# Layer 1: where the two upper halves stand among the involutions and the second convolution

## The chip, the cores and the metric

One Trainium2 chip, one of its cores. The metric is the time of one execution in device microseconds, the median of several runs. Lower is better.

## What is computed

Input `x` has 16 images of 16 channels of 256 x 256 values, in float32. Layer 0 is a spectral operator, layer 1 a convolutional gate; both work on a group-normed input and add their result to it. Only layer 1 is changed:

```python
xs = x.reshape(B * C, 1, H, W)
f = mish(conv2d(xs, W1, b1))                      # 4 features per channel, 3x3
top, bot = (f[:, :, :H2], f[:, :, H2:])           # upper and lower half of the rows
ker = conv2d(relu(conv2d(bot, Wred, bred)), Wspan, bspan)
top_inv = (patches(top) * ker[:, None]).sum(axis=2)   # involution
bo = bot.reshape(B, C, 4, H2, W)
shuffled = concatenate([ti, roll(bo, -1, axis=1)], axis=3)
out = mish(conv2d(shuffled, W2, b2))              # 64 -> 16 channels, 3x3
pooled = out.mean(axis=(2, 3))
gate = sigmoid(Weca[0] * left + Weca[1] * mid + Weca[2] * right)
return x * gate[:, :, None, None]
```

## The kernel before

The program runs layer 0 in three parts and then layer 1 (`layer1`, line 933). The change touches layer 1's main loop alone (lines 1288 to 1329).

**Units.** An image is cut into nine units (`blocks`, line 1268): eight of 30 output rows and eight channels, and a tail of eight rows and all channels. A unit holds up to two groups of four channels; the tail has one. `Unit` has these steps:

- Making it loads its two inputs `z` (lower and upper half) from `zn` in DRAM on SP's queue (`load_rows`, line 1006).
- `lower` (line 1050): per group two matmuls into a PSUM tile `c` (`conv1`, line 1037), and two ScalarE activations into `bot` (line 1056).
- `reduce` (line 1058): four small matmuls into `pr` (line 1064), two ScalarE relus into `r` (line 1073), and the stores of `bot` to `cf` from GpSimd's queue (line 1157).
- `upper(g)` (line 1076), g = 0 and 1: the two matmuls of a group into `c`, and eight ScalarE activations of 32 lanes into `wide` (line 1085). For the tail, `upper(1)` does nothing.
- `spread` (line 1092): eight GpSimd copies inside `wide` (lines 1097, 1098) that need both groups of `upper`.
- `involution(f)` (line 1100), f = 0 to 3: per group one matmul into `pd` (line 1105), then on VectorE one product `t` (line 1113) and two sums `top` (line 1116). `involution(3)` issues the stores of `top` from GpSimd's queue (lines 1127 to 1139).

**Second convolution.** `conv2` (line 1167) treats one of eight slabs of the image before, in pieces between `yield`s; slab s of the image before runs in iteration s. The first piece: eight matmuls `c2ps` from `rows` (line 1185), a ScalarE copy `mid` (line 1199), a VectorE sum `pair` (line 1175). The second: sixteen matmuls from `rows`, VectorE's `even` and `both` (lines 1204, 1206), the rest of `pair`. The third: mish of `even` (line 1196), sixteen matmuls from `pair`, VectorE's `odd` (line 1212). The slab is loaded from `cf` on SP's queue (`conv2_rows`, line 1165) one iteration ahead.

**Gate.** In iteration s = 8, where there is no slab, `gate` (line 1217) makes one small matmul `pg` (line 1237) and an exp on ScalarE (line 1240), then in four steps, in iterations 8, 0, 1 and 2, scales the image on GpSimd (line 1253), with its parts loaded on SP's queue (line 1229) and stored from GpSimd's (line 1262).

**What sets the order.** The section is a manual schedule: PE, ScalarE, VectorE and GpSimd each run their instructions in the order in which the loop writes them. Iteration i works on three units at a time: `now` (unit i, its involutions), `nxt` (unit i + 1, its lower, reduce, upper, spread), and unit i + 2, whose loads are begun.

**PSUM.** Two tiles for `c` (so each `upper` or `lower` group takes the tile of the group two before it), three for `pd`, `pr` and `pg`, one for `c2ps` (in the last image's slabs also the three).

Of the kernel before, what the change touches and what calls it, by code (L numbers as in the profile page):

```python
# [932 lines left out]
def layer1(ctx, tc, d, zn, cf, mr, nb):  # L933
# [228 lines left out]
    def conv2_rows(b, s):  # L1162
        t = rows2[(8 * b + s) % 2]
        flat = cf[b % 4].rearrange("(t y) f c x -> (y f c) t x", y=2)
        nc.sync.dma_start(out=t[:, :, 1 : N + 1], in_=flat[:, 16 * s : 16 * s + 17])
# [106 lines left out]
    def begin_unit(i):  # L1272
        if i < len(order):
            b, s = order[i]
            units[i] = Unit(b, i, *blocks[s])

    E = mybir.EngineType
    with tc.manual_schedule(engines={E.PE, E.Activation, E.DVE, E.Pool}):
        begin_unit(0)
        begin_unit(1)  # L1280
        u = units[0]
        u.lower()
        u.reduce()
        u.upper(0)
        u.upper(1)
        u.spread()
        acc, last, second = None, iter(()), iter(())
        for i in range(9 * nb + 12):
            b, s = divmod(i, 9)
            now, nxt = units.pop(i, None), units.get(i + 1)  # L1290
            begin_unit(i + 2)
            if s == 8 and b < nb:
                conv2_rows(b, 0)
            if s < 7 and b and b <= nb:
                conv2_rows(b - 1, s + 1)
            if nxt:
                nxt.lower()
            next(second, None)
            second = iter(())
            if s == 8 and b and b <= nb:  # L1300
                last = gate(b - 1, acc)
                next(last)
            if s < 8 and b and b <= nb:
                if s == 0:
                    acc = sm.tile([P, 16], F32, tag="acc", name="acc")
                second = conv2(b - 1, s, acc)
            if now:
                now.involution(0)
            next(second, None)
            if nxt:  # L1310
                nxt.reduce()
            if s == 8:
                next(last, None)
            if now:
                now.involution(1)
            next(second, None)
            if nxt:
                nxt.upper(0)
            if now:
                now.involution(2)  # L1320
            if s == 8:
                next(last, None)
            if nxt:
                nxt.upper(1)
                nxt.spread()
            next(last, None)
            next(second, None)
            if now:
                now.involution(3)
# [159 lines left out]
@with_exitstack  # L1489
def forward(ctx, tc, d):  # L1490
    nb = d["x"].shape[0]
    dram = ctx.enter_context(tc.tile_pool(name="dram", bufs=1, space=DRAM))
    keep = ctx.enter_context(tc.tile_pool(name="keep", bufs=1))
    al = dram.tile([NF, 2, 64, nb, N], F32, name="al")
    bd = dram.tile([nb, P, P], F32, name="bd")
    hd = dram.tile([2, 2, 64, nb, C, N], F32, name="hd")
    tabs = (
        dram.tile([P, 2, C, N], F32, name="td"),
        dram.tile([NF, P, 384], F32, name="avd"),
        dram.tile([P, 2, C, N], F32, name="ed"),  # L1500
    )
    zn = dram.tile([nb, N + 2, C, N + 2], F32, name="zn")
    cf = dram.tile([4, N + 2, 4, C, N], F32, name="cf")
    mr = keep.tile([P, nb, G, 2], F32, name="mr")
    layer0_forward(tc, d, al, bd, tabs)
    layer0_mix(tc, d, al, hd, tabs)
    layer0_back(tc, d, hd, bd, zn, mr, tabs[2])
    layer1(tc, d, zn, cf, mr, nb)
# [25 lines left out]
```

## Time and profile before

| what | us |
|---|---|
| median of 3 runs | 7288.94 |
| lowest and highest run | 7282.32, 7289.96 |
| the profiled execution | 7272.96 |
| its span, first to last instruction | 7271.2 |

The span by stages, from an answer of the trace by stretches (busy us of each engine, TensorE's granted clock, share of the DMA engines):

| stretch, us | what runs | PE | VectorE | ScalarE | GpSimd | clock | DMA |
|---|---|---|---|---|---|---|---|
| 0 to 3560 | layer 0 | 3205.66 | 2686.58 | 1558.39 | 1343.08 | 0.98 | 0.48 |
| 3573 to 3790 | layer 1, image 0 | 174.95 | 140.53 | 138.39 | 103.31 | 0.86 | 0.58 |
| 3790 to 4010 | image 1 | 207.22 | 177.73 | 142.09 | 107.38 | 0.98 | 0.82 |
| 4010 to 7050 | images 2 to 15 | 2852.52 | 2449.04 | 1963.48 | 1870.62 | 0.98 | 0.86 |
| 7050 to 7271 | the end, conv2 and gate of the last image | 163.18 | 127.68 | 74.59 | 91.04 | 0.92 | 0.69 |

How to read the lines below: a group line has the line of the kernel, engine, operation, tiles (out<-in), shapes and count, then busy us and mean ns of one, then the idle time of the engine just before and what ended it. A timeline line has start, duration, engine, line, operation, tiles, shapes and count of merged records, and in brackets the idle time before it and who ended it. A float32 matmul leaves two records, so "x4" at line 1037 is one group. A line by stretches has the stretch, its length, busy us and counts of PE, PE's weight loads, VectorE, ScalarE and GpSimd, then clock, DMA share and GB/s. PE is TensorE, DVE VectorE, ACT ScalarE, POOL GpSimd, SP SyncE.

### The profile page before, as it was taken

How to read it: one execution, taken by the hardware profiler on the slowest of the kernel's cores; microseconds unless marked ns; L12 is line 12 of the kernel's file. 1: busy time of each engine (PE TensorE's matmuls, PEld its weight loads, DVE VectorE, ACT ScalarE, POOL GpSimd, SP SyncE). 2: the span in 40 equal slices, each digit the busy share in tenths (PEclk: the TensorE clock that was granted, in tenths of full speed). 3: DMA queues.
4: the chain of work that ended last, by engine and by line, in shares of the span. 5: the costliest groups of instructions: out<-in, count | busy, mean ns of one | idle time of the engine just before them, and what ended most of it. 6: DMA issues, size and time to landing. Idle time of an engine off the chain costs nothing.

```text
span 7271.2 us, 144305 instructions
## 1 busy us (share of the span) xinstructions
PE 6603.5 (91%) x55592; PEld 3651.8 (50%) x55592; DVE 5587.6 (77%) x10106; ACT 3876.9 (53%) x6043; POOL 3524.5 (48%) x4614
## 2 busy tenths in 40 slices
PE   7889999899999998999789999999999999999996
PEld 5767778666666766677423333333333333333332
DVE  8999985466666666788678787788877887778875
ACT  2223333466666665222366666666666666666662
POOL 2334445322222222666555666556665566665663
PEclk9899999999999999999889999999999999999999
DMA  3334444433333332999767888888888889888886
GB/s 100 114 112 125 123 120 125 123 99 99 99 96 99 98 99 87 325 325 326 242 180 225 254 269 249 254 261 258 271 244 252 256 254 275 253 247 260 253 261 229
DMA packets 716081, 1443.39 MB, mean 199 GB/s; under 512 B 98954, under 2 KB 525254, under 8 KB 673638
## 3 DMA queue, kind: packets, MB, share of 16 engines
q1 hardware_dynamic: 567206, 959.76, 44.1%
q0 software_dynamic: 148192, 474.40, 21.1%
q8 instruction: 444, 7.27, 0.4%
q14 instruction: 239, 1.96, 0.1%
HBM read 877.12 MB, written 556.47 MB: 197 GB/s over the span
## 4 chain that ended last, share of the span: by engine, by line
PE 37%; DMA 5%; ACT 4%; DVE 3%; issue 1%; POOL 0%; SPq 0%; DVEq 0%; ACTq 0%; POOLq 0%
PE c2ps L1185 14%; PE c L1037 11%; PE pd L1105 10%; ACT wide L1085 3%; DMA rows<-cf 3%; DVE top L1116 1%; PE pr L1064 1%; DMA z<-zn 1%; DVE t L1113 1%; DMA cf<-bot 0%; SPq L1017 0%; DVE pair L1175 0%; ACT L1085 0%; ACT bot L1056 0%; POOL o L1253 0%
## 5 line engine op out<-in xcount | busy, mean ns | idle before, releaser
L1085 ACT ACTIVATE wide<-c,b 32x512 f32<-32x512 f32 x2176 | 1479.0, 680 | 832.1 <-PE c L1037 768.3
L1116 DVE TENSOR_TENSOR top<-pd,t 32x512 f32<-32x512 f32 x2176 | 1504.1, 691 | 53.0 <-DMA cf<-top 0.5
L1037 PE MATMUL c<-z,w 102*128 102x512 f32 x2048 | 1046.0, 636 | 212.3 <-ACT wide L1085 190.8
L1097 POOL COPY wide<-wide 32x1031 f32<-32x1031 f32 (+1 forms) x576 | 576.0, 1000 | 1167.8 <-ACT wide L1085 1141.7
L1113 DVE TENSOR_TENSOR t<-pd,r 64x512 f32<-64x512 f32 x1088 | 744.5, 684 | 504.5 <-PE pd L1105 472.1
L1105 PE MATMUL pd<-wide,dw 128*128 128x512 f32 x2048 | 1026.4, 622 | 16.4 <-DVE top L1116 11.5
L720 POOL DMA_DIRECT2D hd<-h x512 | 324.4, 640 | 1195.9 <-DVE h L713 1170.9
L1037 PEld LDWEIGHTS c<-z,w 102*128 102x128 f32 x2048 | 384.0, 197 | 818.3 <-issue 488.8
L1185 PE MATMUL c2ps<-rows,c 128*32 128x512 f32 x6144 | 722.9, 603 | 24.6 <-DMA rows<-cf 19.0
L1105 PEld LDWEIGHTS pd<-wide,dw 128*128 128x128 f32 x2048 | 370.3, 194 | 641.6 <-issue 490.5
L1098 POOL COPY wide<-wide 32x1031 f32<-32x1031 f32 (+1 forms) x576 | 573.3, 995 | 33.7
L643 PE MATMUL ps<-tt,lt 128*64 128x256 f32 x4224 | 495.5, 384 | 13.8 <-DMA tt<-td 10.6
L700 PE MATMUL ph<-ix,yt 64*128 64x256 f32 x4128 | 500.9, 390 | 5.6 <-issue 4.8
L313 PE MATMUL px<-wxn,u 128*64 128x256 f32 x4224 | 481.7, 379 | 7.8 <-ACT o L320 7.8
L207 PE MATMUL pu<-fy,eo 128*128 128x128 f32 x2048 | 427.0, 292 | 26.5 <-DVE u L224 21.8
L1185 PEld LDWEIGHTS c2ps<-rows,c 128*32 128x32 f32 x6144 | 176.7, 109 | 533.5 <-issue 400.3
L700 PEld LDWEIGHTS ph<-ix,yt 64*128 64x128 f32 x4128 | 392.3, 190 | 92.0 <-issue 45.0
L873 POOL TENSOR_TENSOR x<-x,o 128x512 f32<-128x512 f32 x256 | 324.3, 1267 | 216.6 <-DVE o L872 197.3
L607 DVE TENSOR_SCALAR alb<-alc,m 128x1024 f32<-128x1024 f32 x330 | 420.2, 1398 | 0.0
L214 PE MATMUL pv<-at,eo 128*128 128x128 f32 x2048 | 413.7, 285 | 0.0
L651 DVE COPY s<-ps 128x512 f32<-128x512 f32 x264 | 265.7, 1024 | 189.0 <-PE ps L643 171.2
L665 PE MATMUL pg<-alb,s 128*32 128x64 f32 x16896 | 274.1, 221 | 132.3 <-issue 86.4
(217 smaller groups left out, 11785.6 us busy)
## 6 DMA issues: line engine op xcount, KB each, us to landing
rows<-cf SPq DMA_DIRECT2D x128, 2176.0 KB
z<-zn SPq DMA_DIRECT2D x768, 257.8 KB
cf<-top POOLq DMA_DIRECT2D x512, 240.0 KB, 7.0
cf<-bot POOLq DMA_DIRECT2D x96, 840.0 KB, 11.4
alc<-al SPq DMA_DIRECT2D x264, 256.0 KB
zn<-zb SPq DMA_DIRECT2D x128, 516.0 KB
o<-zn SPq DMA_DIRECT2D x128, 516.0 KB
z<-in_x SPq DMA_DIRECT2D x64, 1024.0 KB
```

Source lines behind the costliest of these rows:

```text
L207: nc.tensor.matmul(pu[:, xh, e].rearrange("p v m -> p (v m)"), lhsT=lhs, rhs=fy[:, e], start=True, stop=True,)
L313: nc.tensor.matmul(ps[64 * k : 64 * k + 64, :, h], lhsT=u[:, h, part, g0 + j + k].rearrange("p f c -> p (f c)"), rhs=wxn[:, h, part], star ...
L643: nc.tensor.matmul(ps[64 * h : 64 * h + 64, v], lhsT=lt[:, h, k, 1 - v : 3 - v].rearrange("p l f c -> p (l f c)"), rhs=tt[:, h, k], start= ...
L700: nc.tensor.matmul(ph[q][:, e], lhsT=yt[lanes, i].rearrange("p t k -> p (t k)"), rhs=ix[lanes, i], start=n == 0, stop=n == 3,)
L1037: nc.tensor.matmul(ps[:, a], lhsT=w, rhs=z[:k, c : c + 2, 0:N], start=True, stop=True)
L1085: nc.scalar.activation(self.feat[64 - 32 * q : 96 - 32 * q, f, self.groups[g], :H], ps[q][32 * f : 32 * f + 32], AF.Mish, bias=b1[0][32 * ...
L1097: nc.gpsimd.tensor_copy(flat[0:32, f, 1:m], flat[64:96, f, 0 : m - 1])
L1098: nc.gpsimd.tensor_copy(flat[96:128, f, 0 : m - 1], flat[32:64, f, 1:m])
L1105: nc.tensor.matmul(ps, lhsT=dwt if self.tail else dw, rhs=self.feat[:, f, cs, :H], start=True, stop=True,)
L1113: nc.vector.tensor_tensor(t[64:128], ps[:64], self.r[:, cs], ALU.mult)
L1116: nc.vector.tensor_tensor(self.top[32 * f : 32 * f + 32, cs, q], ps[lanes], t[lanes], ALU.add)
L1185: nc.tensor.matmul(ps[32 * j : 32 * j + 32], lhsT=w[:, blk], rhs=src[:, 4 * j + blk : 4 * j + blk + 4, x : x + H], start=(i, blk) == (0, 0 ...
```

## The change

In the loop's body `nxt.upper(0)` moves up, ahead of `now.involution(1)` and with it ahead of the second piece of conv2. `nxt.upper(1)` and `nxt.spread()` move up from behind `now.involution(2)` to ahead of it. Between the two halves there now stand one involution feature and one piece of conv2. The steps and what they compute stay the same.

```diff
             if s == 8:
                 next(last, None)
+            if nxt:
+                nxt.upper(0)
             if now:
                 now.involution(1)
             next(second, None)
             if nxt:
-                nxt.upper(0)
+                nxt.upper(1)
+                nxt.spread()
             if now:
                 now.involution(2)
             if s == 8:
                 next(last, None)
-            if nxt:
-                nxt.upper(1)
-                nxt.spread()
             next(last, None)
             next(second, None)
             if now:
                 now.involution(3)
```

## Prediction

> **What bounds the kernel now.** I read the page first. TensorE (PE) is busy for 91% of the span, and of its groups only `c` (line 1037) waits long for another engine: 190.8 us for ScalarE's `wide` activations (line 1085). Layer 0, which the change doesn't touch, ends near 3560 us.
>
> ```profile
> PE 6603.5 (91%) x55592; PEld 3651.8 (50%) x55592; DVE 5587.6 (77%) x10106; ACT 3876.9 (53%) x6043; POOL 3524.5 (48%) x4614
> L1037 PE MATMUL c<-z,w 102*128 102x512 f32 x2048 | 1046.0, 636 | 212.3 <-ACT wide L1085 190.8
> ```
>
> Then the timeline of layer 1, engine by engine. First a unit in the steady state (PE, then ScalarE): the `c` at 5604.25 is the second half of `upper`, those at 5611.46 and 5614.11 the two groups of the next `lower`. ScalarE needs 11.26 us for the sixteen `wide`; it starts when the first half lands and ends at 5614.06. The second `lower` needs the PSUM buffer of the second half, so PE idles 0.77 us.
>
> ```profile
> 5604.25 1.88 PE L1037 MATMUL c<-z,w 102*128 102x512 f32 x4
> ...
> 5611.46 1.88 PE L1037 MATMUL c<-z,w 102*128 102x512 f32 x4
> 5614.11 1.99 PE L1037 MATMUL c<-z,w 102*128 102x512 f32 x4 [0.77 <-ACT wide L1085]
> ```
> ```profile
> 5602.80 11.26 ACT L1085 ACTIVATE wide<-c,b 32x512 f32<-32x512 f32 x16 [6.00 <-PE c L1037]
> 5614.92 2.47 ACT L1056 ACTIVATE bot<-c,b 128x512 f32<-128x512 f32 x4
> ```
>
> Second, image 0, which has no second convolution yet. The same wait is 0.60 and 3.65 us, and after the long one four matmul records take 3.78 us, not 1.88: PE's clock has halved.
>
> ```profile
> 3634.54 1.88 PE L1105 MATMUL pd<-wide,dw 128*128 128x512 f32 x4
> 3637.03 1.99 PE L1037 MATMUL c<-z,w 102*128 102x512 f32 x4 [0.60 <-ACT wide L1085]
> 3642.67 3.78 PE L1037 MATMUL c<-z,w 102*128 102x512 f32 x4 [3.65 <-ACT wide L1085]
> 3646.24 3.50 PE L1105 MATMUL pd<-wide,dw 128*128 128x512 f32 x4
> 3649.67 1.06 PE L1064 MATMUL pr<-bot,wr 128*32 128x512 f32 x8
> ```
>
> Third, the gate's iteration (s=8): ScalarE loads two tables around the gate's exp and sets the end of this stretch; PE idles 3.60 and 1.86 us.
>
> ```profile
> 4234.59 3.78 PE L1037 MATMUL c<-z,w 102*128 102x512 f32 x4 [3.60 <-ACT wide L1085]
> 4240.23 3.78 PE L1037 MATMUL c<-z,w 102*128 102x512 f32 x4 [1.86 <-ACT wide L1085]
> ```
> ```profile
> 4225.94 0.22 ACT L1240 ACTIVATE gate<-gate 128x16 f32<-128x16 f32 x1
> 4227.63 1.28 ACT L1085 ACT_TABLE_LOAD   x1 [1.47 <-PE c L1037]
> 4228.92 11.25 ACT L1085 ACTIVATE wide<-c,b 32x512 f32<-32x512 f32 x16
> ```
>
> Last, what comes next once PE no longer waits for ScalarE: about three units after a gate PE waits for `rows`, and the DMA engines are full there (the column before the last is their share).
>
> ```profile
> 4324.16 1.97 PE L1185 MATMUL c2ps<-rows,c 128*32 128x512 f32 x16 [0.89 <-DMA rows<-cf]
> ```
> ```profile
> 4304.00:4312.00 8.00, 8.00 (x44) 2.74 (x38) 7.74 (x12) 3.62 (x6) 5.33 (x9) 1.00 1.03 346
> 4312.00:4320.00 8.00, 7.23 (x41) 2.49 (x34) 7.61 (x12) 7.72 (x12) 5.13 (x5) 1.00 0.99 333
> ```
>
> **What the skill says.** TensorE: Matmul & The Clock Gate, Part 1 (the HAM clock gate): activity is judged in free-running windows of 3413 ns, and an idle one halves the clock. The trace agrees: its half-clock stretches last 3.41, 6.83 or 10.24 us, a matmul record then takes 1061 ns against 592, and idle times of 3.6 us bring it while most of about 2.3 us don't. SBUF — State Buffer, two separate sides: VectorE with two SBUF inputs and GpSimd hold a shared port in turn. The trace agrees in part: `pair` (line 1175, 128x1161) takes 1.37 us alone and up to 2.95 us beside the gate's scaling (line 1253), but 1.23 us, its normal time at 128x1032, in 15 cases beside the spread's copies (line 1097). DMA: Bandwidth & Descriptors, queues, rings and completion order: each DMA engine takes packets from its queues in turn, so POOL's stores slow SP's loads. No row shows the turns; the full DMA rows above fit it.
>
> **The change part by part.** No instruction is added or removed. On PE `upper(0)` goes ahead of `involution(1)` and the second piece of conv2; `upper(1)` goes ahead of `involution(2)`. The order on the other engines and queues is unchanged, so no DMA is moved past another; the new names in ScalarE's list are only PSUM tiles.
>
> (1) Steady unit. Counting from `lower`, with issue-to-issue times of the rows (c, pd 1.82; conv2 pieces 1.79, 3.6 and 3.57; pr 0.97): upper(0) at 8.2, pd1 10.0, conv2 11.8, upper(1) 15.4, pd2 17.2, pair products 19.0, pd3 22.6, next lower 24.5. ScalarE runs the first eight `wide` 10.2 to 15.8 and the second 17.4 to 23.1; second `lower` wants its buffer at 26.3, 3.2 us of cover. The 0.77 idle, 0.83 us from issue to issue, goes: 25.37 becomes 24.54. What is late next: `pair` must be summed before its products. VectorE gets even, both, pair after the conv2 piece, 15.55 to 18.1, against 19.0: 0.85 us of cover (2.7 before). The PSUM ring of three for `pd` is free each time (closest: pd1's last at 15.4). So PE alone sets 24.5 us. upper(0) itself meets no new wait: its PSUM tile is freed by `bot`, for which pr, ahead of it, waits anyway. Spread starts 5.4 us earlier in the unit and delays nobody. Value 0.83, bounds 0 (cover of pair lost) and 0.83. Six such units per image.
>
> (2) Unit s=7 (one group in the next): VectorE works without a gap from 4193.81 to 4220.86, so PE's 0.65 us wait only changes place. Nothing, 0.1 us either way.
>
> (3) Image 0. The loop that sets its period of 23.9 us: second `lower` 3.57, pd0 3.44, pr 0.99, pd1 2.62, upper(0) 1.98, `wide` 11.25. Now pd1 is out of it (2.62), and since VectorE's 8 x 2.145 = 17.2 us fills the wait, PE's idle time shrinks to about 1 us and the clock stays up (1.85 + 1.72 off the two slow rows). 23.9 - 2.62 - 3.57 = 17.7, just over VectorE's 17.2. Six iterations x 6.2 = 37 us; at least 16 if the clock still halves. Its s=8: one pd group, 1.0.
>
> (4) Gate iteration, 14 that a further image follows: upper(0) no longer stands behind pd1, so the table load follows exp at once: the 1.47 idle goes, 1.4 us. The idle and half clock after it stay, since eleven us of `wide` still end last.
>
> (5) Image 1 (units 10 to 15): no gate, `rows` land over 20 us ahead. 6 x 0.83 = 5.
>
> (6) Images 2 to 15. By the trace's packet records the `rows` of the fourth slab (s=3) land 0.6 to 1.3 us before their use in eleven of fourteen, about the least from landing to matmul; that load is thus already bound. It stands behind two gate loads on SP, which wait for the gate's store, which POOL issues after the spread, one block of tail stores and the next spread: POOL is busy in that whole stretch, so it moves only by the 1.4 of (4). Later POOL stores come 4 to 6 us earlier and push it back by an estimated 0.7. PE, 1.4 + 3 x 0.83 = 3.9 us earlier, waits for it: 3.2 us more than its 1.6 on average, with pr, upper(0) and pd1 queued behind, so ScalarE and VectorE stand still too. An idle of 4.8 us halves the clock for a window: 1.7 us, four times in five. Then three units at 0.83. So 0.7 + 2.5 - 1.4 = 1.8 for a bound image, 1.4 + 5.0 = 6.4 for one that isn't. Eleven and three: 39 us. Bounds 14 x 6.4 = 90 and 0.
>
> Sum: 37 + 1 + 5 + 39 = 82, against the profiled 7272.96 us (span 7271.2): 7191. That execution is 16 us under the median of the runs, 7288.94; from there 7207.
>
> **Rivals.** Full gain: DMA is never in the way, 37 + 1 + 5 + 90 = 133, time 7156. For it: the mean DMA share is 0.86, and units s=5 to 7 have landing times to spare. Against: the saturated rows. Chance 0.22. Nothing after image 1: `rows` move back as much as PE moves up and the clock falls each time; 43 us, 7246. For it: a 4.25 us wait for `rows` at 5444 did halve the clock. Chance 0.2. No effect: pair's 0.85 us cover is lost to the port in every unit (1.23 becomes 2.9 us, 0.8 of stall) and image 0 stays at half clock, together -16 us or less; 15 rows beside the copies speak against. Chance 0.03. Slower: the earlier POOL stores hold the fourth slab back by 4 us beyond its time of before, and two half-clock windows (3.4 us) follow: -4 - 3.4 + 2.5 = -4.9 an image, 14 x 4.9 = 69 against 43, so 26 slower, 7315. It decides once the delay passes 2.2 us (then 14 x 3.1 = 43). Against it: the stores that move up ended before that load did anyway. Chance 0.04.
>
> **How the numbers follow.** The forecast has 0.51. Range 7150 to 7250: full gain below, nothing after image 1 above. 0.2% is 14.6 us, about what a measurement of this kernel can tell from no change. Faster: 0.51 + 0.22 + 0.2 = 0.93; same 0.03; slower 0.04.
>
> **What would show it.** (1) no 0.77 waits at line 1037, unit 24.5 us; (3) image 0's period 17.7 us and no half clock; (4) table load straight after exp; (6) waits of `c2ps` for `rows` of some 5 us at s=3, with half-clock rows behind. I am wrong if `c2ps` waits for `pair`, or if the fourth slab lands earlier or later than 1 us around its old place.

## The result, and the profile after

The changed kernel takes 7213.30 us (median of 4 runs, 7206.87 to 7223.74), the kernel before 7285.63 (4 runs, the first three and one beside the changed kernel). The ratio is 0.9905, with a 95% interval of 0.9887 to 0.9923: some 69 us less. The profiled execution of the changed kernel was its longest, 7223.74 us, and layer 1 begins in it at 3581.31 us, 8.25 us later than in that of before; layer 0 is the same code, so I compare within layer 1. From the first matmul of layer 1 to the span's end it is 3698.1 us before and 3640.7 after, some 57.4 less.

The page: PE's share is the same, but the wait for `wide` at line 1037 has halved, and line 1185 has a wait for `rows` that it hardly had. The single line below is line 1185 before.

```profile
PE 6585.2 (91%) x55592; PEld 3670.2 (51%) x55592; DVE 5553.1 (77%) x10106; ACT 3882.2 (54%) x6043; POOL 3517.7 (49%) x4614
L1037 PE MATMUL c<-z,w 102*128 102x512 f32 x2048 | 1017.7, 629 | 122.9 <-ACT wide L1085 100.9
L1185 PE MATMUL c2ps<-rows,c 128*32 128x512 f32 x6144 | 743.3, 617 | 100.8 <-DMA rows<-cf 96.1
```
```profile
L1185 PE MATMUL c2ps<-rows,c 128*32 128x512 f32 x6144 | 722.9, 603 | 24.6 <-DMA rows<-cf 19.0
```

A steady unit in the timeline of the changed kernel, PE and then ScalarE. The two groups of `lower` now stand in one line of eight records without a wait, and from `pd` at 5466.80 to the next, 5472.05, nothing is idle. ScalarE works in two blocks, one for each half of `upper`, and ends the second at 5467.29, before `lower` starts.

```profile
5452.33 1.99 PE L1037 MATMUL c<-z,w 102*128 102x512 f32 x4
...
5459.59 1.99 PE L1037 MATMUL c<-z,w 102*128 102x512 f32 x4
...
5466.80 1.98 PE L1105 MATMUL pd<-wide,dw 128*128 128x512 f32 x4
5468.62 3.60 PE L1037 MATMUL c<-z,w 102*128 102x512 f32 x8
5472.05 1.88 PE L1105 MATMUL pd<-wide,dw 128*128 128x512 f32 x4
```
```profile
5454.41 5.62 ACT L1085 ACTIVATE wide<-c,b 32x512 f32<-32x512 f32 x8 [0.47 <-PE c L1037]
5461.67 5.62 ACT L1085 ACTIVATE wide<-c,b 32x512 f32<-32x512 f32 x8 [1.64 <-PE c L1037]
```

A repeating iteration of image 0 on PE: the 3.65 us wait is now 1.14, VectorE holds PE for 1.05 us elsewhere, and no four records take 3.78 us any more. (At the two ends of image 0, at 3597.63 and 3764.66, they still do.)

```profile
3655.18 1.10 PE L1105 MATMUL pd<-wide,dw 128*128 128x512 f32 x2 [1.05 <-DVE top L1116]
3656.11 1.88 PE L1037 MATMUL c<-z,w 102*128 102x512 f32 x4
3659.13 1.98 PE L1037 MATMUL c<-z,w 102*128 102x512 f32 x4 [1.14 <-ACT wide L1085]
3660.95 1.88 PE L1105 MATMUL pd<-wide,dw 128*128 128x512 f32 x4
```

The gate's iteration, ScalarE: the second table load follows the exp at once. PE still waits twice.

```profile
5523.67 0.22 ACT L1240 ACTIVATE gate<-gate 128x16 f32<-128x16 f32 x1
5523.91 1.28 ACT L1085 ACT_TABLE_LOAD   x1
5525.20 11.25 ACT L1085 ACTIVATE wide<-c,b 32x512 f32<-32x512 f32 x16
```
```profile
5530.87 2.43 PE L1037 MATMUL c<-z,w 102*128 102x512 f32 x4 [3.06 <-ACT wide L1085]
5536.51 3.78 PE L1037 MATMUL c<-z,w 102*128 102x512 f32 x4 [3.20 <-ACT wide L1085]
```

The same image a hundred microseconds later, PE and then the stretches: the fourth slab is waited for 5.55 us, the sixteen records behind it take 3.33 us where they took 1.97, and before it the DMA engines are full.

```profile
5621.55 3.33 PE L1185 MATMUL c2ps<-rows,c 128*32 128x512 f32 x16 [5.55 <-DMA rows<-cf]
5624.70 1.03 PE L1064 MATMUL pr<-bot,wr 128*32 128x512 f32 x8
```
```profile
5602.00:5610.00 8.00, 8.00 (x43) 2.73 (x42) 7.12 (x10) 6.16 (x10) 5.39 (x7) 1.00 1.00 322
5610.00:5618.00 8.00, 6.00 (x14) 2.28 (x13) 6.82 (x10) 3.43 (x8) 7.43 (x11) 1.00 1.06 260
```

The trace's packet records (the `rows` are the 1 KB packets of SP's queue, 2176 a slab) and the instruction times, set against the gate matmul `pg` of each image, give this table. It holds means over images 2 to 15, for the last column over the 12 periods from `pg` to `pg` of images 3 to 14; it is used for all runs below. The wait is PE's idle time before the slab's first matmul.

| us after `pg` | gate stores of s=1 | of s=2 | fourth slab issued | landed | in flight | used | wait | image period |
|---|---|---|---|---|---|---|---|---|
| before | 76.8, 81.1 | 101.9, 106.4 | 78.6 | 98.5 | 19.8 | 100.5 | 1.3 | 224.0 |
| after | 72.6, 76.6 | 94.6, 98.1 | 77.3 | 99.7 | 22.4 | 100.7 | 6.2 | 223.1 |

So PE, freed of ScalarE, is ready for the fourth slab 4.7 us earlier (the use less the wait: 94.5 instead of 99.2 us after `pg`) but gets it no earlier than before. The period's gain of 0.9 us leaves out the first and the last image; over all fourteen periods it is 1.2 (223.8 and 222.6). One image weighs much in the means of before: in image 14 the slab landed at 87.1, twelve us ahead of its use. Without image 14 the landing is 99.3 before and 99.4 after, and the flight 20.4 and 22.1.

Where the 57.4 us came from: from layer 1's first matmul to the 3.65 us wait that opens image 1 (3793.25 before, 3764.66 after) 220.2 us became 183.4, 36.8 less; image 1, from there to the same place an image later, 222.85 became 214.9, 8.0 less; the thirteen images after that 2912.0 became 2898.0, 14.0 less; what follows, image 15 and the end, gave back 1.4.

### The profile page after: what moved, and what is told of

Same layout as the page of the kernel before. It is cut to its first block, busy times and chain, and to the rows that moved or that the text cites. A ratio compares the mean times of both kernels' runs of the same rounds, so it can differ in the third digit from the quotient of the medians.

```text
span 7222.0 us, 144350 instructions
## 1 busy us (share of the span) xinstructions
PE 6585.2 (91%) x55592; PEld 3670.2 (51%) x55592; DVE 5553.1 (77%) x10106; ACT 3882.2 (54%) x6043; POOL 3517.7 (49%) x4614
## 4 chain that ended last, share of the span: by engine, by line
PE 38%; DMA 7%; ACT 3%; DVE 1%; SPq 1%; issue 1%; POOL 0%; DVEq 0%; POOLq 0%; ACTq 0%
PE c2ps L1185 14%; PE c L1037 11%; PE pd L1105 11%; DMA rows<-cf 5%; ACT wide L1085 2%; DMA z<-zn 2%; PE pr L1064 2%; SPq L1017 0%; DVE top L1116 0%; ACT r L1073 0%; ACT L1240 0%; ACT L1085 0%; POOL o L1253 0%; DVE t L1113 0%; DVE pair L1175 0%
## 5 line engine op out<-in xcount | busy, mean ns | idle before, releaser
L1037 PE MATMUL c<-z,w 102*128 102x512 f32 x2048 | 1017.7, 629 | 122.9 <-ACT wide L1085 100.9
L1105 PE MATMUL pd<-wide,dw 128*128 128x512 f32 x2048 | 993.4, 607 | 12.5 <-DVE top L1116 11.0
L1185 PE MATMUL c2ps<-rows,c 128*32 128x512 f32 x6144 | 743.3, 617 | 100.8 <-DMA rows<-cf 96.1
L1056 ACT ACTIVATE bot<-c,b 128x512 f32<-128x512 f32 x544 | 344.4, 684 | 470.7 <-issue 382.2
```

The lines of the kernel that those rows point to most:

```text
L1037: nc.tensor.matmul(ps[:, a], lhsT=w, rhs=z[:k, c : c + 2, 0:N], start=True, stop=True)
L1105: nc.tensor.matmul(ps, lhsT=dwt if self.tail else dw, rhs=self.feat[:, f, cs, :H], start=True, stop=True,)
L1185: nc.tensor.matmul(ps[32 * j : 32 * j + 32], lhsT=w[:, blk], rhs=src[:, 4 * j + blk : 4 * j + blk + 4, x : x + H], start=(i, blk) == (0, 0 ...
```

## The experiments

My theory after the result: the gain in image 0 and 1 is the wait for ScalarE; in the later images it is swallowed by the fourth slab, which comes late because SP's gate loads wait for gate stores ahead of it (SP order) and because the stores, now earlier, are under way at the same time and slow it (shared DMA). The runs below ask how much is due to each. The rival: the later images gain their part and image 0 little.

**The change in image 0 alone.** Run `img0`, the old order wherever b > 0 (shown in part, against the changed kernel; `upper(1)` and `spread` go the same way):

```diff
+            early = b == 0
-            if nxt:
+            if nxt and early:
                 nxt.upper(0)
...
+            if nxt and not early:
+                nxt.upper(0)
```

> The new order in the iterations of image 0 alone, the old one elsewhere. My working of the sum: image 0 gives some 36 us of the 69 (trace: 36.8 up to the first matmul of image 1's lower), so the ratio to before is 0.9950, some 7250 us. Rival, that the gain comes mainly from the 0.77 us waits of the later images: then this gives under 15 us (0.998).

Measured, as the ratio to before with its 95% interval: 0.9953 (0.9940 to 0.9965), 7243.38 us. That is 34 us (25 to 44), half of the whole gain. In its waits of PE the long list for `wide` is still there, 128 times against 38 after the change:

```profile
PE c L1037 <- ACT wide L1085: 170.9, 128, 4.0
```

So the iterations of one image in sixteen bring half the gain, and the rival falls.

**Six buffers for the gate's parts.** Runs `after_o6` and `before_o6`, each kernel with one number changed; a gate load then takes a buffer whose store ended long ago.

```diff
-    op = ctx.enter_context(tc.tile_pool(name="l1o", bufs=4))
+    op = ctx.enter_context(tc.tile_pool(name="l1o", bufs=6))
```

> The changed kernel with six buffers instead of four for the gate's image parts, so that the gate's loads on SP never wait for the gate's stores. Theory SP order (the fourth slab of rows stands on SP's queue behind gate loads that wait for gate stores): rows of s=3 are issued and land over 5 us earlier, the mean wait of 6.2 us falls under 1, no half clock there, and an image takes some 217.5 us instead of 223.0: 14 x 5.5 = 77 us less than the changed kernel, ratio to before 0.980. Theory shared DMA (the engines are full in this stretch, and gate stores that came earlier take turns with the slab's load): the issue comes earlier but the bytes ahead of it stay, it lands 1 to 3 us earlier, wait 3 to 5 us, 15 to 40 us less than the changed kernel, ratio 0.985 to 0.988.

> The kernel before with six buffers for the gate's image parts, the control of after_o6. Theory SP order: its mean wait of 1.3 us for rows at s=3 goes, 14 x 1.3 = 18 us plus one half clock, ratio 0.997. Theory shared DMA: half of that or nothing, 0.998 to 1.000. In neither does it gain as much as after_o6, since ScalarE's 0.77 us wait stays in each unit.

Measured: `after_o6` 0.9753 (0.9740 to 0.9767), 7097.93 us; `before_o6` 0.9964 (0.9951 to 0.9976), 7253.28 us. In `after_o6` the fourth slab is issued at 66.2 us after `pg`, 11.1 earlier, lands at 80.9 and is used at 94.5 without a wait. The landing is 18.8 us earlier than in the changed kernel, where theory shared DMA had 1 to 3. Line 1185 of the page has no wait for `rows` left:

```profile
L1185 PE MATMUL c2ps<-rows,c 128*32 128x512 f32 x6144 | 721.8, 602 | 5.6 <-DVE odd L1212 5.6
```

The image takes 214.4 us; in `before_o6` 222.8. With `rows` out of the way, then, the reordering is worth 8.4 us an image, not about one. This one number moves the kernel before by 26 us (1 - 0.9964) and the changed one by about 111 (0.9905 - 0.9753). SP order is shown: the loads and stores are all still there, and with the flight of the changed kernel the slab would have landed at 66.2 + 22.4 = 88.6 us, still ahead of its use at 94.5, so the earlier issue is enough to end the wait. It is not all that changed: the flight fell too, to 14.7 us, and to 14.0 in `before_o6`, where the gate stores go out when they did before (77.1 and 81.4).

**The gate stores put back.** Run `late_store`: the changed kernel, its gate step in s=1 and s=2 written behind `involution(3)`; SP's order stays.

```diff
-            next(last, None)
+            if s not in (1, 2):
+                next(last, None)
             next(second, None)
             if now:
                 now.involution(3)
+            if s in (1, 2):
+                next(last, None)
```

> The changed kernel, but the gate's scaling and stores of iterations s=1 and s=2 are written behind involution(3), so that POOL stores them about where it did before the change; SP's order is the same. Theory shared DMA: the fourth slab, no longer beside these stores, lands 1 to 2.5 us earlier (99.7 back to 97.5 us after pg), mean wait 6.2 falls to about 4, 20 to 40 us less than the changed kernel, ratio 0.985 to 0.988. Theory SP order: its issue time is the same, so wait and time are too, ratio 0.990.

Measured: 0.9826 (0.9813 to 0.9840), 7155.24 us, more than either theory gave. The gate stores of s=1 go out at 75.1 and 78.7, those of s=2 at 95.9 and 100.2. The slab is issued at 76.8, 0.5 earlier than in the changed kernel, but lands at 95.7, 4.0 earlier: in flight 18.9 us against 22.4. PE's wait falls from 6.2 to 2.9 us and the image to 217.5. From 4010 to 7000 us of its trace:

```profile
PE c2ps L1185 <- DMA rows<-cf: 41.5, 13, 6.0
```

against this in the changed kernel, from 4010 to 7050:

```profile
PE c2ps L1185 <- DMA rows<-cf: 93.6, 18, 10.7
```

So shared DMA holds too: with nearly the same issue time the flight depends on when POOL stores. Whether the transfers slow each other in the DMA engines or in DRAM no run here tells. The run moves the stores of both iterations at once, and with them the unit's own stores ahead of them on POOL's queue, so which of these counts most stays open.

**The bytes of the gate stores.** Run `cut_store`:

```diff
-                nc.gpsimd.dma_start(out=dst.rearrange("c y x -> y c x"), in_=o[:, :, 1 : N + 1])
+                nc.gpsimd.dma_start(
+                    out=dst.rearrange("c y x -> y c x")[:, :1], in_=o[:, :1, 1 : N + 1]
+                )
```

> The changed kernel, storing one of each part's four channels of the gated image; three quarters of the output are left out, its loads and its scaling are all there. Theory shared DMA: with the stores' bytes gone from the stretch, the fourth slab lands at least 5 us earlier, its 6.2 us wait falls under 1 us, and the time is near that of the kernel with six part buffers, 0.975 to 0.980. Theory SP order alone (the wait for the stores and not their bytes): gate loads are let go only 2 to 3 us earlier, since a smaller store lands that much sooner after the same issue; the wait falls to 3 or 4 us, 0.984 to 0.987.

Measured: 0.9738 (0.9723 to 0.9753), 7092.91 us. The slab is issued at 70.8 (6.5 earlier, since a smaller store frees its buffer sooner), lands at 87.1 (in flight 16.4) and is never waited for; an image takes 214.4 us, as in `after_o6`. The 12.6 us by which it lands earlier are 6.5 of issue and 6.1 of flight: both mechanisms, about equally.

**Each half of the change alone.** Run `first_only`, the kernel before with `upper(0)` ahead of `involution(1)`; run `second_only`, with `upper(1)` and `spread` behind `upper(0)`.

```diff
+            if nxt:
+                nxt.upper(0)
             if now:
                 now.involution(1)
             next(second, None)
-            if nxt:
-                nxt.upper(0)
```
```diff
             if nxt:
                 nxt.upper(0)
+                nxt.upper(1)
+                nxt.spread()
...
-            if nxt:
-                nxt.upper(1)
-                nxt.spread()
```

> The kernel before with upper(0) alone moved ahead of involution(1); upper(1) and spread stay behind involution(2). Theory ScalarE's start (the wait of the second lower goes because ScalarE begins its sixteen activations earlier, at the first half): the second half's activations still end some 1.4 us before the second lower wants its buffer, so the 0.77 us waits go, a unit falls from 25.4 to some 24.3 us, and with GpSimd's stores 1.8 us later than in the changed kernel the fourth slab of rows lands a little earlier: ratio to before 0.987 to 0.991. Theory that both moves are needed: waits of about 0.77 us stay, image 0 alone gains, ratio 0.995 to 0.998.

> The kernel before with upper(1) and spread alone moved ahead of involution(2), straight behind upper(0), which stays. Theory ScalarE's start: it begins at the same time and its sixteen activations end at the same time, so the 0.77 us waits stay and the unit takes 25.4 us: ratio 0.998 to 1.002. Theory that upper(1)'s place sets the wait: as the changed kernel, 0.990.

Measured: `first_only` 0.9878 (0.9860 to 0.9895), 7198.53 us; `second_only` 0.9993 (0.9983 to 1.0002), 7275.88 us. PE's wait at `lower` in a steady unit of `second_only`, which the timeline of `first_only` has nowhere in such a unit:

```profile
5494.50 1.88 PE L1037 MATMUL c<-z,w 102*128 102x512 f32 x4
5497.14 1.98 PE L1037 MATMUL c<-z,w 102*128 102x512 f32 x4 [0.76 <-ACT wide L1085]
```

And over the whole of `first_only`:

```profile
PE c L1037 <- ACT wide L1085: 102.4, 38, 4.0
PE c2ps L1185 <- DMA rows<-cf: 84.9, 19, 9.1
```

Both lines are close to those of the changed kernel (100.9 us in 38 waits for `wide`, 96.1 in 19 for `rows`). What counts is when ScalarE can start its sixteen activations, which is `upper(0)`'s place; that of `upper(1)` adds nothing that these runs can tell.

**A version that beats both.** Run `gate_late_o6`: `after_o6`, with the gate's sum and exp behind the unit's activations.

```diff
             if nxt:
                 nxt.reduce()
-            if s == 8:
-                next(last, None)
-            if nxt:
                 nxt.upper(0)
...
                 nxt.spread()
+            if s == 8:
+                next(last, None)
             if now:
                 now.involution(2)
-            if s == 8:
+            if s < 8:
                 next(last, None)
-            next(last, None)
             next(second, None)
             if now:
                 now.involution(3)
+            if s == 8:
+                next(last, None)
+                next(last, None)
```

> The changed kernel with six part buffers, and in the gate's iteration the sum over the image and the exp written behind upper(1) and spread, the gate's remaining steps behind involution(3). ScalarE then does the sixteen activations before the exp and its two table loads. If ScalarE's chain sets that stretch, the second lower gets its buffer some 2.4 us earlier an image, 14 x 2.4 = 34 us less than after_o6, ratio to before 0.971. Against: the table loads then stand ahead of the next bot activations and may hold up reduce by as much, ratio 0.975.

Measured: 0.9693 (0.9680 to 0.9706), 7062.88 us. An image takes 212.0 us, 2.4 less than in `after_o6`, as worked out. ScalarE in that iteration:

```profile
5449.36 11.24 ACT L1085 ACTIVATE wide<-c,b 32x512 f32<-32x512 f32 x16 [0.60 <-PE c L1037]
5460.61 1.28 ACT L1240 ACT_TABLE_LOAD   x1
5461.91 0.22 ACT L1240 ACTIVATE gate<-gate 128x16 f32<-128x16 f32 x1
5462.14 1.28 ACT L1056 ACT_TABLE_LOAD   x1
5463.44 2.42 ACT L1056 ACTIVATE bot<-c,b 128x512 f32<-128x512 f32 x4
```

The sixteen activations stand ahead of the two table loads, which now fall where PE has `lower` to do.

## Why the prediction was right, and where its terms were off

7207 was predicted and 7213.3 measured, inside the range. The waits that go and the wait that takes their place were named rightly; but two terms were off in opposite directions, and the closeness is in part luck.

(1) Steady unit: the 0.77 us wait went and `c2ps` never waits for `pair` in a way that counts (0.3 us in images 2 to 15). The unit takes 24.28 us (`c2ps` at 5449.58 to 5473.86), not 24.54, so the term is 1.10 us, not 0.83. I had summed the old issue distances; back to back the two groups of `lower` take 3.43 us, less than twice 1.82. `first_only` and `second_only` show that ScalarE's start is the cause. The prediction leaned on 15 rows in which `pair` (128x1032) was not slowed beside the spread's copies; in the new order, beside copies of both lines 1097 and 1098, it takes up to 1.68 us instead of 1.22. The 0.46 us more are within the 0.85 us of cover.

(2) Unit s=7: 0.1 us shorter, as said.

(3) Image 0: 18.0 us an iteration (3641.12 to 3659.13) against 17.7 predicted, and no half clock. The term with its two ends was 38; the traces give 36.8, the run with image 0 alone 34.

(4) Gate iteration: the table load follows the exp, and the first gate stores come at 21.8 instead of 23.2 us after `pg`, 1.4 earlier. Right.

(5) Image 1: 8.0 us with the gate iteration behind it, against 5 + 1.4; the rest is the larger unit gain.

(6) Images 2 to 15, the step that failed in size: the price of POOL's earlier stores. I wrote that SP's chain "moves only by the 1.4 of (4)"; the slab's issue moved by 1.4. But I wrote that later POOL stores "push it back by an estimated 0.7"; its flight grew by 2.6 us, 19.8 to 22.4, so that on average it landed 1.2 later and not 0.7 earlier, just past the 1 us that I had named as a sign of being wrong. Without image 14 the issue moved by 1.6, the flight grew by 1.6 and the landing stayed. So the price is 1.6 to 2.6 us instead of 0.7. The mechanism was right (`late_store`, with nearly the same issue, brings the flight to 18.9). The wait became 6.2 us, predicted 4.8; the half clock behind it came in 13 of the 14 images, and from this slab's use to the next takes 26.5 us, 2.2 over the free unit, with 0.5 of a further wait in it. An image gained 0.9 us (1.2 over all fourteen), where 39 over 14 is 2.8. Without the wait the change would have brought 8.4 us an image (`after_o6` against `before_o6`), so the fourth slab took back some 7.5 us of it.

The sum by parts, 36.8 + 8.0 + 14.0 - 1.4 = 57.4 in the profiled pair, is below 82, and its shortfall is (6). The medians of the runs differ by 72 us. Part of the closeness of 7207 to 7213 is thus the spread between executions (7206.87 to 7223.74) and not the sum. And within an image two errors met: an unhindered image gains 8.4 us instead of 6.4, but the slab takes back 7.5 instead of 3.6. That the first made up for half of the second is luck.

Of the rivals, full gain needed `rows` out of the way: `after_o6` reaches it, and passes the 7156 worked out for it, because the unit's gain was larger and image periods shrink by the 1.3 us wait of before as well. The slower end needed a slab 2.2 us later with two half-clock windows; it came 1.2 later, or not at all later without image 14. "Nothing after image 1" had 0 where the forecast had 39 for (6): the 14.0 less 1.4 of the profiled pair lies nearer to this rival. What PE gains ahead of the slab is lost in the wait for it, and a half clock follows, as the rival had it; but the slab hardly moved back, and the units behind it do gain.

## What to carry to other kernels

When an engine's wait is removed in a loop, look for the load that lands just in time: here the slab landed about a microsecond before its use in eleven of fourteen images, and that was the next bound, worth some 7.5 of the 8.4 us an image. A load's landing has two prices, when its queue lets it go (what waits ahead of it there) and what is under way beside it, and an edit that speeds up the stores can raise the second. Two more buffers, dull beside a reordering, were worth 26 us before it and about 111 after it.

## What the runs showed of the hardware that was not expected

A load of 2.2 MB on SP's queue was in flight 14.0 us (`before_o6`), 14.7 (`after_o6`), 16.4 (`cut_store`), 18.9 (`late_store`), 19.8 (before) and 22.4 us (after), with the same packets each time. By the packet records all queues together moved 4.2, 4.4, 5.1, 6.0, 6.1 and 6.6 MB in these flights, in each run 295 to 316 GB/s, with the DMA engines busy for 97% of the flight or more on average. The flight is thus about the bytes that go out in it over 300 GB/s. The part that differs most is POOL's stores, 1.0 MB in `before_o6` and 3.1 MB after. A longer flight also meets more stores, so these figures alone don't show which comes first; `late_store` and `cut_store`, which change the stores, do.

A wait of 5.55 us halved PE's clock although PE had been busy for most of the unit before it: the sixteen records that took 1.97 us took 3.33, so that a wait for DMA was charged about a quarter more than its own length.

The prediction read the clock a little too simply. Three half-clock stretches of layer 1 before lasted 13.65 us, and of 15 idle times of 2.0 to 2.5 us at full clock in the program before (from 150 us on), 8 were followed by a half clock within 4 us. In the trace every change of the clock falls on one grid of 3413 ns, and between 150 and 7000 us of the kernel before each full-clock stretch of this grid with PE busy for less than 42% of it was followed by the half clock, and none with more than 46%. In the changed kernel the two overlap from 41% to 52%. So here the length of an idle time alone does not decide, but how much of it falls into one stretch of the grid.
